# Attention B on features normalized ahead, its projections drained by ScalarE, with new starting ranks for all stages

## Chip, core and metric

The kernel runs on one core of a Trainium2 chip. The metric is the device time of one execution in microseconds (us); the kernel before has a median of 1521.22 us over three runs (1521.19 to 1521.49). The engines are called by the profile's names: PE is TensorE (matmuls, with PEld for its weight loads), DVE is VectorE, ACT is ScalarE, POOL is GpSimd, SP is SyncE, which issues the DMAs.

## The reference

The input x is 4 x 2048 x 256 in float32. Four blocks follow one another, each as x = x + block(layernorm(x)): attention A, the FFN, attention B, and the FFN again. What matters here is attention B, where S (4 here) is its sequence and the 2048 positions are its batch:

```python
k = (src @ Wk_w.T + Wk_b).reshape(S, B, n, -1)
v = (src @ Wv_w.T + Wv_b).reshape(S, B, n, -1)
q = (inp @ Wq_w.T + Wq_b).reshape(S, B, n, -1)
k = unitnorm(k); q = unitnorm(q)
w = sigmoid(src @ Ww_w.T + Ww_b)
A = einsum('sbnq,sbnv->bnvq', k, v * w[:, :, :, None])
r = sigmoid(inp @ Wr_w.T + Wr_b)
out = einsum('sbnq,bnvq->sbnv', q, A) * r[:, :, :, None]
out = out.reshape(S, B, d) @ Wo_w.T + Wo_b
```

with n = 16 heads of 16 numbers. The FFN is 256 to 704 to 256 with silu, and its inputs, weights and hidden values are all rounded blockwise to a 4-bit grid. Attention A divides by norms taken over the whole tensor, so a first pass over all of x has to end before its main pass can begin.

## The kernel before, in words

The 2048 positions are cut into 16 groups of 128 (one position per partition). A group holds its four sequence steps s side by side, `x` [128, 4, 256], and a tile is one (group, s). Each group goes through `attention_a`, `ffn_in` and four `ffn_tile` for the first FFN, `attention_b`, then `ffn_in` and four `ffn_tile` for the second.

Ahead of the groups, `first_pass` loads all x once, takes moments of each tile with `bn_stats` (L653, into a tile `moments` of its own, with sums in `both`), normalizes on ScalarE into four borrowed tiles `XN`, and lets TensorE sum the products of features over all of x (L551). It also loads and prepares the weights: `center` (L903 to L921) subtracts from a weight matrix its mean over the input features. To do so it multiplies the matrix by ones on TensorE (L910), and VectorE subtracts the result divided by 256 from both halves (L916). With centered weights, the mean of x need not be subtracted from x.

Attention B uses this. It takes the sums and variances of x, lets GpSimd work out the reciprocal deviation rstd (`root`, six steps of `take_rstd`; the FFN takes two more for a shift `off`), and transposes the raw x on TensorE (`turn`, L1122, copied out by ScalarE in L1129). For each tile, `project` (L1145) multiplies it by the centered `wqkB` (512 columns) and `wvgB` (288 columns: values and two gates) into two PSUM banks. VectorE drains both in L1528 as bank x rstd + bias, into `qk` and `vg`; the biases lie on all partitions in `bqkB` and `bvgB`, loaded by SP (L484). Then VectorE multiplies all pairs (L1546) and sums over heads (L1553), ScalarE squares (L1577), gates and roots follow, GpSimd weighs the values (L1654), VectorE adds them (L1672, L1675), and the result is turned and projected by `woB`. The bias of the last projection is added to x by GpSimd ahead (L1494), after the transposes have read x.

The FFN tile is TensorE's largest piece: hidden products (L1363), a silu on ScalarE (L1384), the product on VectorE (L1395), the blockwise rounding (`quantize`: VectorE L384, L385, L389, L402, L405, ScalarE L395 and L1192, GpSimd L1220), transposes (L1418, copied by L1430) and the down projection (L1441). `ffn_in` has, for the whole group, `root`, four normalizations on ScalarE (L378) into `xn`, the same rounding, and `turn`. The sums that a next layernorm needs come with the additions to x (L339), and the variances from ScalarE (L345).

The order is written by a planner in the kernel (`Plan`). Each operation is registered with an engine, an estimated duration, a rank, and tokens that it reads and writes. `plan.order(2)` then plays the engines forward in time. Whenever an engine is free, it gets the ready operation of the lowest rank whose buffers are to be had. An operation marked `port=True` is not started while the other of VectorE and GpSimd runs such a one. The result is a fixed instruction order for each engine. `BEGIN` (L1078) gives every group six starting ranks, for attention A, `ffn_in` and tiles of the first FFN, attention B, `ffn_in` and tiles of the second. Buffers come from pools: four banks for hidden products (`mm`), four others (`bank`) for everything else that TensorE writes, eight x, six `turned`, one `qk`, two `vg`. `given` takes a buffer out of a pool for the first pass and returns it after its last user.

Of the kernel before, what the change touches and what calls it, by code (L numbers as in the profile page):

```python
# [18 lines left out]
P = 128  # L19
# [230 lines left out]
def kernel(  # L250
# [56 lines left out]
    def load_x(dst, j):  # L307
# [10 lines left out]
    bqkB = one([P, 2 * D], "bqkB")  # L318
    bvgB = one([P, NV], "bvgB")
# [4 lines left out]
    norm_tiles = {k: one([P, NJ, 6, S], f"norms_{k}") for k in ("a", "f1", "b", "f2")}  # L324


    moments = one([P, NJ, S, 6], "moments")
    both = one([P, NJ, S, 2], "both")
    norms = {
        (k, j): [t[:, j, n, :] for n in range(6)]  # L330
# [26 lines left out]
    def take_rstd(key, step):  # L357
        sums, var, y, off, v, t = norms[key]
        if step == 0:
            nc.gpsimd.tensor_scalar(v, var, 1.0 / D**3, LN_EPS, ALU.mult, ALU.add)  # L360
        elif step == 1:
            power(v, y, nhalf[:, 0, :])
        elif step == 2:
            nc.gpsimd.tensor_mul(t, y, y)
        elif step == 3:
            nc.gpsimd.tensor_mul(t, t, v)
        elif step == 4:
            nc.gpsimd.tensor_scalar(t, t, -0.5, 1.5, ALU.mult, ALU.add)
        elif step == 5:
            nc.gpsimd.tensor_mul(y, y, t)  # L370
        elif step == 6:
            nc.gpsimd.tensor_mul(off, sums, y)
        else:
            nc.gpsimd.tensor_scalar(off, off, -1.0 / D, 0.0, ALU.mult, ALU.add)
# [55 lines left out]
    tiles("tok", 1, [P, S, D], fp)  # L430
    tiles("vz", 2, [P, S, 2 * D], bp)
# [12 lines left out]
    def first_pass():  # L444
# [5 lines left out]
        for b in XN:  # L450
            nc.gpsimd.memset(b.ap[:, :, D : D + 1], 1.0)
        WQK, PROD, WNAT = (plan.given("pp", 0) for _ in range(3))
# [4 lines left out]
        wnat = WNAT.ap.rearrange("p (t c) d -> p t c d", t=2)  # L457
        MK, GROW, MAPT, G = (plan.given(p, 0) for p in ("vz", "tok", "sc", "fac"))
# [32 lines left out]
        for at, token, fn in (  # L491
# [23 lines left out]
            (34.1, ("bB", 0), over_rows(bqkB[:, :D], b_bq)),  # L515
            (34.2, ("bB", 0), over_rows(bqkB[:, D:], b_bk)),
            (34.3, ("bB", 0), over_rows(bvgB[:, :D], b_bv)),
            (34.4, ("bB", 0), over_rows(bvgB[:, D : D + NH], b_br)),
            (34.5, ("bB", 0), over_rows(bvgB[:, D + NH :], b_bw)),
# [54 lines left out]
        def roots(js):  # L574
# [3 lines left out]
            half = [moments[:, js, :, 3 * i + 1 : 3 * i + 3] for i in range(2)]  # L578
            total = both[:, js]
# [45 lines left out]
        for ns in together:  # L625
            for n in ns:
# [21 lines left out]
                for s in range(S):  # L648
# [5 lines left out]
                            moments[:, j, s, :], xj[:, s, :]  # L654
                        ),
                        [(X, s)],
                        [("moments", j, s)],
# [5 lines left out]
            seen = [("moments", i, s) for i in js for s in range(S)]  # L663
# [239 lines left out]
        def center(at, w, n, tokens):  # L903
# [10 lines left out]
            def dve():  # L914
                for c in range(KC):
                    nc.vector.scalar_tensor_tensor(  # L916
                        w[:, c, :], mm.ap[:, :n], -1.0 / D, w[:, c, :], ALU.mult, ALU.add
                    )

            op("PE", 0.2 + n / 290.0, at, pe, tokens, [(mm, 0)])  # L920
            op("DVE", 0.2 + n / 450.0, at + 2, dve, [(mm, 0)], tokens)  # L921
# [16 lines left out]
        center(AHEAD + 50.0, wqkB, 2 * D, [("wqkB", 0)])  # L938
        center(AHEAD + 54.0, wvgB, NV, [("wvgB", 0)])
# [139 lines left out]
        (-91, -18, -64, 57, -73, -13),  # L1079
        (35, 82, 59, 126, 299, 228),  # L1080
        (293, 397, 356, 450, 375, 486),
        (370, 404, 412, 488, 580, 596),
        (433, 471, 475, 573, 630, 638),
        (485, 530, 525, 621, 687, 715),
        (518, 567, 530, 673, 716, 745),
        (588, 644, 630, 743, 560, 676),
        (602, 669, 606, 752, 637, 771),
        (671, 699, 702, 801, 719, 886),
        (714, 797, 826, 891, 958, 1069),
        (788, 865, 877, 996, 972, 1083),  # L1090
        (839, 971, 923, 1030, 822, 1063),
        (879, 1027, 930, 1059, 1017, 1130),
        (910, 1041, 830, 1087, 873, 1230),
        (953, 1023, 1012, 1151, 918, 976),
    ]

    def group(j):
# [7 lines left out]
        def xs(s):  # L1105
            return X.ap[:, s, :]
# [56 lines left out]
        def root(at, key):  # L1163

            n = 6 if key[0] == "b" else 8
# [321 lines left out]
        def attention_b(at):  # L1487
            key = ("b", j)
            root(at, key)
            xT = turn(at, X, range(S), lambda: X.ap)  # L1490

            def bias():
# [8 lines left out]
                at + 3,  # L1501
# [6 lines left out]
            for s in range(S):  # L1508
                a, b = plan.buf("bank"), plan.buf("bank")
                rstd = norms[key][2][:, s : s + 1]  # L1510
                for bank, n, w, bvec, dst, us, ds, name in (
                    (a, 2 * D, wqkB, bqkB, qk, 1.73, 0.7, "wqkB"),
                    (b, NV, wvgB, bvgB, vg, 0.98, 0.46, "wvgB"),
# [10 lines left out]
                        "DVE",  # L1524
                        ds,
                        at + 5 + 3 * s,
                        lambda bank=bank, n=n, bvec=bvec, dst=dst, s=s, rstd=rstd: (
                            nc.vector.scalar_tensor_tensor(  # L1528
                                dst.ap[:, s, :],
                                bank.ap[:, :n],  # L1530
                                rstd,
                                bvec,
                                ALU.mult,
                                ALU.add,
                            )
                        ),
                        [(bank, 0), (key, "rstd"), ("bB", 0)],
# [236 lines left out]
```

## Time and profile before

| | us |
|---|---|
| median of three runs | 1521.22 |
| the profiled execution: its time | 1523.6 |
| the profiled execution: span from the first to the last instruction | 1521.6 |
| granted TensorE clock, mean share | 0.997 |
| POOL busy in the span | 693.2 |
| DMA moved | 27.68 MB, mean 18 GB/s |

The profile is of one execution. Its page lists for each engine the busy time, its share of the span and the count of instructions. The span is also cut into 40 equal slices of 38 us, with the busy share in tenths (9 is 90% or more). In the groups of instructions, L12 is line 12 of the kernel, and `qk<-bank` means that `qk` is written and `bank` read. After the shapes stand the count, the busy time of the group, the mean ns of one, and the idle time of the engine just before these instructions, with what ended it. Matmuls are pipelined and their ends are modelled, so TensorE's busy time is more than its work; the distance between starts tells what one costs. A float32 matmul appears as two instructions.

### The profile page before, as it was taken

To read this page: it belongs to the slowest core of one execution; us is meant where nothing else is said; L and a number is where in the kernel's file an instruction comes from. 1 tells how busy PE (TensorE), PEld (TensorE's weight loads), DVE (VectorE), ACT (ScalarE), POOL (GpSimd) and SP (SyncE) were. 2 spreads that over 40 slices of the span, in tenths; PEclk is the share of its full clock that TensorE was granted. 3 is DMA by queue.
4 is the path that set the end of the run, shared out by engine and by line. 5 is a ranking of instruction groups with operands and counts; after the bars stand their busy time and mean duration, and the time that the engine had idled before them with its cause. 6 is when DMAs were issued, how large, how long until landed. Compare 5 with 4: busy or idle time off the path is not lost.

```text
span 1521.6 us, 18780 instructions
## 1 busy us (share of the span) xinstructions
PE 1499.4 (99%) x6362; PEld 1073.0 (71%) x6362; DVE 1387.3 (91%) x2266; ACT 810.1 (53%) x1745; POOL 693.2 (46%) x750
## 2 busy tenths in 40 slices
PE   7989999999999999999999999999999999999999
PEld 6847676766767666677667676776677677667777
DVE  6899999899899998989999999898989899999985
ACT  6666455555636556455554455465654455445443
POOL 5444454444536254444543543544453644553531
PEclk9999999999999999999999999999999999999999
DMA  8300000000000000000000000100000000000000
GB/s 268 100 1 1 1 1 0 29 0 11 18 4 7 18 4 5 8 4 22 4 18 8 8 21 14 42 5 4 5 7 1 0 1 1 5 11 14 14 22 21
DMA packets 29025, 27.68 MB, mean 18 GB/s; under 512 B 3585, under 2 KB 28673, under 8 KB 28929
## 3 DMA queue, kind: packets, MB, share of 16 engines
q1 hardware_dynamic: 28928, 26.49, 5.6%
q8 instruction: 50, 0.82, 0.2%
q14 instruction: 47, 0.38, 0.1%
HBM read 18.09 MB, written 8.39 MB: 17 GB/s over the span
## 4 chain that ended last, share of the span: by engine, by line
PE 80%; DVE 15%; issue 2%; ACT 1%; DMA 1%; POOL 0%; SPq 0%; DVEq 0%; POOLq 0%; ACTq 0%
PE bank L1363 32%; PE bank L1441 19%; PE bank L1145 18%; PE bank L1418 5%; PE bank L1122 3%; PE bank L551 2%; DVE h L1395 1%; DVE sh L384 1%; DVE pp L1546 1%; DVE qa L402 1%; DVE sc L1553 1%; DVE qa L389 1%; DVE qa L405 1%; DVE fac L1586 1%; DVE qk L1528 1%
## 5 line engine op out<-in xcount | busy, mean ns | idle before, releaser
L1363 PE MATMUL bank<-wguT,turned 128*128 128x352 f32 x2048 | 637.7, 459 | 0.3 <-DVE h L1395 0.3
L1363 PEld LDWEIGHTS bank<-wguT,turned 128*128 128x128 f32 x2048 | 379.7, 190 | 193.8 <-issue 11.7
L1220 POOL TENSOR_TENSOR qa<-qa,sh 128x704 f32<-128x704 f32 x128 | 203.0, 1586 | 407.6 <-DVE qa L405 315.6
L1441 PE MATMUL bank<-wdT,hqT 128*128 128x256 f32 x1536 | 350.6, 380 | 0.4 <-DVE x L1473 0.4
L1441 PEld LDWEIGHTS bank<-wdT,hqT 128*128 128x128 f32 x1536 | 289.5, 190 | 55.6 <-issue 4.5
L1430 ACT COPY hqT<-bank 128x512 f32<-128x512 f32 (+1 forms) x256 | 114.5, 479 | 94.6 <-PE bank L1418 92.4
L1384 ACT ACTIVATE sil<-bank 128x352 f32<-128x352 f32 x256 | 116.1, 458 | 88.9 <-PE bank L1363 83.5
L395 ACT ACTIVATE qm<-qa 128x704 bf16<-128x704 f32 (+1 forms) x136 | 105.9, 781 | 106.4 <-DVE qa L389 103.4
L1395 DVE TENSOR_TENSOR h<-sil,bank 128x352 f32<-128x352 f32 x256 | 128.8, 508 | 19.1 <-PE bank L1363 11.3
L1654 POOL TENSOR_TENSOR pp<-vg,sc 128x1024 f32<-128x1024 f32 x64 | 131.0, 2066 | 31.8 <-DVE tok L1675 27.1
L402 DVE SCALAR_TENSOR_TENSOR qa<-qm,qa 128x704 f32<-128x704 bf16 (+1 forms) x136 | 125.5, 924 | 12.0 <-ACT qm L395 11.9
L389 DVE SCALAR_TENSOR_TENSOR qa<-sh,h 128x704 f32<-128x704 f32 x128 | 126.7, 994 | 2.2
L1145 PE MATMUL bank<-wvz,turned 128*128 128x512 f32 x256 | 119.4, 604 | 5.5 <-ACT turned L1129 4.0
L405 DVE SCALAR_TENSOR_TENSOR qa<-qm,qa 128x704 f32<-128x704 bf16 (+1 forms) x136 | 122.1, 898 | 3.0
L384 DVE TENSOR_REDUCE sh<-h 128x44 f32<-128x748 f32 x128 | 119.1, 931 | 3.7
L1145 PE MATMUL bank<-wqkB,turned 128*128 128x512 f32 x256 | 119.6, 593 | 0.0
L1129 ACT COPY turned<-bank 128x512 f32<-128x512 f32 x160 | 86.8, 588 | 58.3 <-PE bank L1122 58.1
L1418 PEld LDWEIGHTS bank<-ident,qa 128*128 128x128 f32 x768 | 90.7, 141 | 29.0 <-issue 12.0
L1220 POOL TENSOR_TENSOR qax<-qax,sx 128x1024 f32<-128x1024 f32 x32 | 68.3, 2135 | 87.2 <-DVE qax L405 81.8
L1418 PE MATMUL bank<-ident,qa 128*128 128x128 f32 x768 | 105.0, 273 | 1.2 <-POOL qa L1220 1.1
L1192 ACT ACTIVATE sh<-sh 128x44 f32<-128x44 f32 x128 | 30.6, 239 | 119.2 <-DVE sh L384 116.3
L1145 PEld LDWEIGHTS bank<-wvz,turned 128*128 128x128 f32 x256 | 47.2, 193 | 54.3 <-issue 41.5
(180 smaller groups left out, 2150.1 us busy)
## 6 DMA issues: line engine op xcount, KB each, us to landing
x<-in_L_attn_a_x_dram SPq DMA_DIRECT2D x23, 512.0 KB, 5.5
out_dram<-x SPq DMA_DIRECT2D x64, 128.0 KB, 1.7
hqT<-in_L_ffn_w_down_dram SPq DMA_DIRECT2D x2, 352.0 KB, 3.9
hqT<-in_L_ffn_w_gate_dram SPq DMA_DIRECT2D x5, 128.0 KB, 3.9
hqT<-in_L_ffn_w_up_dram SPq DMA_DIRECT2D x5, 128.0 KB, 2.7
x<-in_L_attn_a_x_dram SPq DMA_DIRECT2D x4, 128.0 KB, 2.3
pp<-in_L_attn_a_Wq_dram SPq DMA_DIRECT2D x2, 256.0 KB, 5.6
pp<-in_L_attn_a_Wk_dram SPq DMA_DIRECT2D x2, 256.0 KB, 5.2
```

Of the source, the lines that this page charges most:

```text
L384: nc.vector.tensor_reduce(amax, src, AX.X, ALU.max, apply_absolute_value=True)
L389: nc.vector.scalar_tensor_tensor(blocks(a), over_blocks(rs), -6.0 * BELOW, src, ALU.mult, ALU.mult)
L402: nc.vector.scalar_tensor_tensor(a, m, FLOOR, a, ALU.max, ALU.add)
L405: nc.vector.scalar_tensor_tensor(a, m, FLOOR, a, ALU.max, ALU.subtract)
L1145: nc.tensor.matmul(bank.ap[:, :n], lhs.ap[:, c, s * P : (s + 1) * P], w[:, c, :], start=(c == 0), stop=(c == KC - 1),)
L1220: lambda: nc.gpsimd.tensor_mul(blocks(a.ap), blocks(a.ap), over_blocks(q.ap[:, 1, :])),
L1363: nc.tensor.matmul(bank.ap[:, :HF], xqT.ap[:, c, s * P : (s + 1) * P], w[:, c, cols], start=(c == 0), stop=(c == KC - 1),)
L1384: lambda g=g, sil=sil: nc.scalar.activation(sil.ap, g.ap[:, :HF], AF.Silu),
L1395: lambda u=u, sil=sil, half=half: nc.vector.tensor_mul(h.ap[:, half * FB // 2 : (half + 1) * FB // 2, :BLK], blocks(sil.ap), blocks(u.ap[: ...
L1418: nc.tensor.transpose(bank.ap[:, (i - i0) * P : (i - i0 + 1) * P], qa.ap[:, HC[i] : HC[i] + P], ident,)
L1441: nc.tensor.matmul(o.ap[:, :D], hqT.ap[:, i, :], wdT[:, i, :], start=(i == 0), stop=(i == 5),)
L1654: nc.gpsimd.tensor_mul(pv.ap.rearrange("p t (n e) -> p t n e", e=HD), vg.ap[:, :, :D].rearrange("p t (n e) -> p t n e", e=HD), over_blocks ...
```

## The change

In attention B, ScalarE first normalizes the group's four tiles into a new buffer `xh` (a pool of one). The shift has 1 added to it, so each normalized row has a mean of one. `turn` reads `xh` in place of x. `root` has eight steps here too, as the shift is needed.

`center` now puts the biases into the weights of attention B: the bias, divided by 256 like the mean, is added to every row of the centered matrix. As the features sum to 256, the product contains the bias once. This takes one more VectorE instruction in each of two calls. The bias tiles become buffers lent from the pools `turned` and `fac` for the first pass. The banks of the two projections then need nothing but a copy, and ScalarE makes it in place of VectorE.

To make room in SBUF, the moments of the first pass lie in columns of the fourth borrowed tile, the one of pool `qk`, that its features leave free, and the norm tiles of all layers but the first are shared by groups j and j + 8. The table `BEGIN` has other numbers throughout.

```diff
-    norm_tiles = {k: one([P, NJ, 6, S], f"norms_{k}") for k in ("a", "f1", "b", "f2")}
-    moments = one([P, NJ, S, 6], "moments")
-    both = one([P, NJ, S, 2], "both")
+    norm_tiles = {
+        k: one([P, NJ if k == "a" else NJ // 2, 6, S], f"norms_{k}") for k in ("a", "f1", "b", "f2")
+    }
...
-            nc.gpsimd.tensor_scalar(off, off, -1.0 / D, 0.0, ALU.mult, ALU.add)
+            nc.gpsimd.tensor_scalar(
+                off, off, -1.0 / D, 1.0 if key[0] == "b" else 0.0, ALU.mult, ALU.add
+            )
...
+    tiles("xh", 1, [P, S, D], fp)
...
+        MOMENTS = XN[3]
+        def moments(js):
+            row, first, n = js.start // 4, js.start % 4, js.stop - js.start
+            assert first + n <= 4
+            return [
+                MOMENTS.ap[:, row, at + S * k * first : at + S * k * (first + n)].rearrange(
+                    "p (j s k) -> p j s k", s=S, k=k
+                )
+                for at, k in ((D + 8, 6), (D + 8 + 4 * S * 6, 2))
+            ]
...
+        BIAS, BIAS2 = (plan.given(p, 0) for p in ("turned", "fac"))
+        bqkB = BIAS.ap[:, 0, :]
+        bvgB = BIAS2.ap.rearrange("p i n -> p (i n)")[:, :NV]
...
-        def center(at, w, n, tokens):
+        def center(at, w, n, tokens, bias=None):
...
             def dve():
+                less, part = mm.ap[:, :n], -1.0 / D
+                if bias:
+                    less, part = bias[0], 1.0 / D
+                    nc.vector.scalar_tensor_tensor(
+                        less, mm.ap[:, :n], -1.0, less, ALU.mult, ALU.add
+                    )
                 for c in range(KC):
                     nc.vector.scalar_tensor_tensor(
-                        w[:, c, :], mm.ap[:, :n], -1.0 / D, w[:, c, :], ALU.mult, ALU.add
+                        w[:, c, :], less, part, w[:, c, :], ALU.mult, ALU.add
                     )
...
-        center(AHEAD + 50.0, wqkB, 2 * D, [("wqkB", 0)])
-        center(AHEAD + 54.0, wvgB, NV, [("wvgB", 0)])
+        center(AHEAD + 50.0, wqkB, 2 * D, [("wqkB", 0)], (bqkB, BIAS))
+        center(AHEAD + 54.0, wvgB, NV, [("wvgB", 0)], (bvgB, BIAS2))
...
     BEGIN = [
-        (-91, -18, -64, 57, -73, -13),
-        (35, 82, 59, 126, 299, 228),
-        (293, 397, 356, 450, 375, 486),
...
-        (910, 1041, 830, 1087, 873, 1230),
-        (953, 1023, 1012, 1151, 918, 976),
+        (-180, -233, -93, -411, -178, -161),
+        (30, -17, 75, 47, 270, 251),
+        (165, 222, 216, 279, 209, 381),
...
+        (818, 610, 806, 933, 837, 1624),
+        (833, 730, 831, 1007, 156, 703),
     ]
...
-            n = 6 if key[0] == "b" else 8
+            n = 8
...
         def attention_b(at):
             key = ("b", j)
             root(at, key)
-            xT = turn(at, X, range(S), lambda: X.ap)
+            xh = plan.buf("xh")
+            for s in range(S):
+                op(
+                    "ACT",
+                    0.52,
+                    at + 1.0 + 0.1 * s,
+                    lambda s=s: normalize(xh.ap[:, s, :], xs(s), key, s),
+                    [(X, s), (key, "rstd")],
+                    [(xh, s)],
+                )
+            xT = turn(at + 1.5, xh, range(S), lambda: xh.ap)
...
-                at + 3,
+                at + 6,
                 bias,
...
                     op(
-                        "DVE",
+                        "ACT",
                         ds,
                         at + 5 + 3 * s,
-                        lambda bank=bank, n=n, bvec=bvec, dst=dst, s=s, rstd=rstd: (
-                            nc.vector.scalar_tensor_tensor(
-                                dst.ap[:, s, :],
-                                bank.ap[:, :n],
-                                rstd,
-                                bvec,
-                                ALU.mult,
-                                ALU.add,
-                            )
+                        lambda bank=bank, n=n, dst=dst, s=s: nc.scalar.copy(
+                            dst.ap[:, s, :], bank.ap[:, :n]
                         ),
-                        [(bank, 0), (key, "rstd"), ("bB", 0)],
+                        [(bank, 0)],
                         [(dst, s)],
                     )
```

The planner's durations for the two drains go from 0.7 and 0.46 us to 0.5 and 0.31. The loads of the biases (L484) keep their ranks and their places in the list.

## Prediction

> **What bounds the kernel now.** I read the page's first two parts, then TensorE's own waits, the stages, and the starts of single matmuls.
>
> The page's busy times and its 40 slices:
>
> ```profile
> PE 1499.4 (99%) x6362; PEld 1073.0 (71%) x6362; DVE 1387.3 (91%) x2266; ACT 810.1 (53%) x1745; POOL 693.2 (46%) x750
> ...
> PE   7989999999999999999999999999999999999999
> ```
>
> TensorE is busy in every slice, but ends of matmuls are modelled, so I count its work by the distance from one start to the next. The chain gives 48 matmuls of L1363 in 14.20 us (296 ns each) and 12 of L1441 in 2.59 us (216). In the timeline a 512-wide one starts every 429 ns, a 288-wide one every 243, a 128-wide one every 109, and the first pass's pair (257 and 129 wide) every 329. With the counts of the groups: 2048 x 296 = 606; 1536 x 216 = 332; 526 x 429 = 226; 260 x 243 = 63; 260 x 216 = 56; some 1470 x 109 = 160; 128 x 329 = 42; 1 for the smallest; in all 1486 us. The first matmul starts at 9.96 us, the last ends at 1518.5 of 1521.6, which is 3.1 before the end. So 1521.6 = 10.0 + 1486 + 3.1 + 22.4, and only the 22.4 us lost between matmuls is open to a better order. The same subtraction by stretch puts 4.1 of it in 0 to 40 us, 0.5 in 40 to 80, 8.3 in 80 to 120 and 9.5 in all the rest.
>
> TensorE's waits (total, times, longest) say on whom:
>
> ```profile
> PE bank L551 <- ACT vg L378: 10.0, 1, 10.0
> PE bank L1145 <- ACT turned L1129: 4.0, 1, 4.0
> PE bank L1418 <- POOL qa L1220: 1.1, 2, 0.6
> PE bank L1122 <- DVE x L339: 0.6, 1, 0.6
> PE bank L1145 <- DVE x L339: 0.5, 1, 0.5
> ```
>
> The 10.0 is the start: loads, moments, first normalized tile. The 4.0 is one wait at 108 us, while the first groups fill the machine. The others are short, and stand behind VectorE or behind GpSimd, which stands behind VectorE. The stages (columns: length, then busy time with count of TensorE, its weight loads, VectorE, ScalarE, GpSimd, then the clock) show who was late:
>
> ```profile
> 80.00:120.00 40.00, 35.28 (x108) 17.96 (x107) 37.06 (x68) 26.67 (x56) 21.12 (x27) 0.91 0.00 1
> 120.00:1480.00 1360.00, 1356.58 (x5709) 968.64 (x5708) 1265.07 (x1980) 722.08 (x1557) 629.85 (x613) 1.00 0.03 9
> ```
>
> From 80 to 120 us VectorE is busy 37.1 of 40, and the clock falls to 0.91: after the 4.0 us wait the next 512-wide matmuls start 850 to 1010 ns apart instead of 429, which costs as much again. The first matmuls of all, at 10 to 15 us, are slow in the same way; most of the first 4.1 us is that and stays. The Trainium skill ("TensorE: Matmul & The Clock Gate", section "What's actually happening") says that the array falls to half its clock after an idle window of about 3.4 us and needs a busy one of that length to come back. The rows agree; by that rule a long wait costs double and many short ones only themselves.
>
> So the floor of any reordering is 10.0 + 1486 + 3.1 + about 3.5 = 1502.6 us of span, 19 below now.
>
> **The change, part by part.**
>
> *VectorE loses two drains per tile.* The two forms of L1528:
>
> ```profile
> L1528 DVE SCALAR_TENSOR_TENSOR qk<-bank,norms_b,bqkB 128x512 f32<-128x512 f32 x64 | 46.8, 737 | 13.9 <-PE bank L1145 13.6
> L1528 DVE SCALAR_TENSOR_TENSOR vg<-bank,norms_b,bvgB 128x288 f32<-128x288 f32 x64 | 32.1, 503 | 3.6 <-PE bank L1145 1.8 <-POOL norms_f L372 1.0 <-POOL norms_b L370 0.2
> ```
>
> 46.8 + 32.1 = 78.9 us go, less 1.1 for one extra instruction in each of two `center` calls (681 and 446 ns, the rows of L916). Busy falls from 1387 to 1310, 91% to 86%. From 120 to 1480 us VectorE's idle time rises from 95 to about 174 us. None of it is on the path by itself: the matmuls cover it.
>
> *ScalarE takes them, and four normalizations per group.*
>
> ```profile
> L1129 ACT COPY turned<-bank 128x512 f32<-128x512 f32 x160 | 86.8, 588 | 58.3 <-PE bank L1122 58.1
> L378 ACT ACTIVATE xn<-x,norms_f 128x256 f32<-128x256 f32 x128 | 68.6, 593 | 31.3 <-POOL norms_f L374 25.8 <-DVE qax L389 5.6
> ```
>
> 64 x 588 = 37.6; the 288-wide copy lies between L1430's 373 ns (256 wide) and L822's 474 (384), about 398, so 64 x 398 = 25.5; 64 x 593 = 38.0. That is 101 us by duration. In sequence they start closer (four normalizations take 2.07 us), so about 85 us more busy: 895 us, 59%. Cost on the path: nothing, while ScalarE has 638 us idle between 120 and 1480.
>
> *GpSimd takes two more steps per group's root*, 16 x 2 x about 0.32 = 10 us (mean of L372 and L374), 46% still. Hidden. TensorE's matmuls keep count and shape. The bias loads keep size and number; but the last one, issued at 53.4 us and landing 2.6 later, is now needed by the last `center`, whose matmuls start at 63.3 us: 7 us in hand, so 0, and at worst the same 7 us if SP's queue slips. Moments in another tile: same instructions, 0 (up to 0.4 us each if a load arrives behind it).
>
> *A wait is added.* Attention B's transposes read raw x now, behind VectorE's last sum. After the change they wait for variance (0.5 + 0.2 us), eight root steps (2.95 us from first to last at 100.6) and four normalizations (2.07), some 5.7 us. Behind a late transpose TensorE's whole queue stands. Ends: 0, and 16 x 5.7 = 91 us with no cover; there is no end below 0, since this wait relieves nobody. I take 0. The nearest row is the FFN input, which has this very chain and quantization after it 32 times, and all idle time before its transposes is:
>
> ```profile
> L1122 PE MATMUL bank<-ident,qax 128*128 128x128 f32 x256 | 34.8, 278 | 0.6 <-DVE x L339 0.6
> ```
>
> The cover is other groups' FFN tiles: eight x buffers, each group's FFN tiles some 32 us of matmuls per layer.
>
> *The order is remade.* BEGIN has new numbers everywhere, so every engine's order changes, and no row prices that. Bounds: 19 us better (the floor) and, the other way, the 91 above.
>
> What I take: the 9.5 us lost after 120 us falls by two thirds, 6 us, since nearly all of it stands behind VectorE, whose slack there nearly doubles; the 8.3 of the fill is VectorE-bound too, but no attention B runs there, so I credit 1 us. 1521.6 - 7 = 1514.6 of span. The profiled execution took 1523.6 us outside a span of 1521.6; the median of the runs is 1521.2, 0.4 under that span. So 1514.2, **1514 us**.
>
> **A rule that speaks against it.** Laying the two engines' records side by side, 45 of 64 `vg` drains and 44 of 64 `qk` drains had GpSimd at work for over half their time, and took the same (501 against 509, 736 against 737 ns). L389, with both inputs in SBUF, took 1190 ns there against 892 without. So the drains that go are work that lost nothing to GpSimd, and what stays, does. The Trainium skill ("SBUF — State Buffer", section "SBUF: two separate sides") gives the reason: a VectorE instruction with two SBUF inputs and a GpSimd instruction lock each other out of a shared port pair. By that rule the 79 us freed can only partly be used, the late stalls stay, and the sum would be 1521.
>
> **Rivals.**
> 1. *The fill goes too.* If the new order leaves no wait over 1 us between 80 and 120 us, the clock stays up, and about 8 us more go: 1514 - 8 = 1506. For it: one wait makes it all. Against: VectorE has 2.9 us idle in those 40.
> 2. *The change buys nothing that TensorE can use.* VectorE's and GpSimd's shared instructions bind as before, the waits move but keep their sum: 1521. For it: the long SBUF instructions and GpSimd's 693 us are untouched. Against: non-contending work (L384, L1395) is plentiful and can fill in.
> 3. *Slower: the transposes of attention B come late.* The normalizations queue in ScalarE behind a table load (1283 ns), a square (1056) and copies, and TensorE stands. One such delay is about 1 us per group; 16 groups, 16 us; less the 6 gained, 1531. It decides from 7/16 = 0.44 us per group. One wait of 4 us, with the slow clock behind it, counts 8. For it: ScalarE's 85 us more, in strict order with 58 table loads. Against: the 0.6 us above.
>
> **How the numbers follow.** Forecast (1510 to 1518) 0.41; rival 1 (1503 to 1510) 0.16; rival 2 (1518 to 1525) 0.15; rival 3 (1525 to 1545) 0.28. The last is taken to 1531, its price; together with the bottom left out below 1504 that leaves under 2 in 10. Range 1504 to 1531. This kernel's measurement can tell 0.2%, 3 us, from no change. Faster by more: rival 1 and all of the forecast, 0.57; within: 0.14; slower: 0.29.
>
> **What would show it.** Right: VectorE at 1310, ScalarE at 895, TensorE's waits after 120 us under 4 us in total, the sum of starts still 1486. Step by step: no idle time before `bank<-ident,xh` over 1 us in all; ScalarE's copies of `qk` and `vg` at 588 and 398 ns. Wrong: a TensorE wait on the normalizations or on `turned` of 2 us or more, a clock under 0.97 in a slice after 120 us, or more table loads than 58. What would break the forecast above all is the fill: its wait can double or go, 8 us either way, and nothing in this profile fixes it.

## The result, and the profile after

The kernel after takes 1524.02 us (median of 22 runs, 1522.12 to 1526.70), the kernel before 1521.57 us beside it (22 runs). The ratio is 1.0016 with an interval of 1.0009 to 1.0022: a faster kernel is excluded, and the loss of 2.5 us is smaller than the 0.2% that the prediction took as its measure. One of the 22 runs of before lay far off, at 2266.8 us, and is not in the ratio.

The profiled execution took 1523.4 us, its span is 1521.3. The first two parts of the page after, to be held against the same lines of before:

```profile
PE 1499.4 (99%) x6362; PEld 1072.7 (71%) x6362; DVE 1345.6 (88%) x2140; ACT 894.8 (59%) x1937; POOL 709.1 (47%) x782
...
PE   7999999999999999999999999999999999999999
```

The work has moved as the diff says: 126 instructions fewer on VectorE, 192 more on ScalarE. TensorE's waits after (total, times, longest) have a new list:

```profile
PE bank L570 <- ACT vg L378: 8.3, 2, 8.0
PE bank L1173 <- DVE wvz L1076: 2.4, 1, 2.4
PE bank L1173 <- ACT turned L1157: 2.1, 2, 1.9
PE bank L1446 <- POOL qa L1248: 1.5, 3, 1.1
PE bank L1446 <- ACT vg L1564: 0.9, 2, 0.7
...
PE bank L1446 <- ACT hqT L1458: 0.5, 1, 0.5
PE bank L1446 <- ACT qk L1564: 0.4, 1, 0.4
```

In place of one wait of 4.0 us in the fill stand two, of 2.4 (at 72 us) and 1.9 (at 113 us). The short waits on VectorE's additions to x are gone, and the FFN's transposes (L1446, L1418 before) wait for ScalarE's copies instead. The stages after (columns as in the prediction):

```profile
80.00:120.00 40.00, 37.69 (x117) 18.19 (x116) 37.83 (x73) 25.29 (x56) 21.58 (x33) 1.00 0.02 8
120.00:1480.00 1360.00, 1355.29 (x5711) 969.05 (x5710) 1222.99 (x1853) 808.74 (x1750) 645.35 (x639) 1.00 0.03 9
```

From 80 to 120 us TensorE is better off, but after 120 us it has 1.3 us less busy time, although VectorE has 42 us more idle time there.

The prediction's ledger can be drawn up for every run: for each matmul the distance to the next start, less the usual distance of its shape (the one that it has when nothing delays it, 296 ns for 352 columns). The sum of these usual distances is about 1485.5 us in every kernel here, the tail 3.2. What differs (us):

| run | first matmul | lost 0-40 | 40-120 | after 120 | VectorE busy | span | time, median | ratio to before, interval |
|---|---|---|---|---|---|---|---|---|
| before | 10.0 | 4.2 | 8.9 | 9.6 | 1387 | 1521.6 | 1521.57 | |
| b_again | 8.3 | 4.7 | 8.1 | 9.7 | 1388 | 1519.8 | 1521.8 | |
| after | 8.0 | 5.1 | 8.1 | 11.1 | 1346 | 1521.3 | 1524.02 | 1.0016, 1.0009-1.0022 |
| a_again | 8.5 | 4.8 | 9.9 | 11.9 | 1346 | 1524.1 | 1526.2 | |
| b_act_drain | 7.9 | 5.0 | 7.9 | 8.5 | 1339 | 1518.3 | 1520.50 | 0.9993, 0.9984-1.0002 |
| a_dve_drain | 8.4 | 4.4 | 7.7 | 51.4 | 1409 | 1560.8 | 1562.78 | 1.0273, 1.0259-1.0287 |
| b_seed0 | 8.1 | 4.7 | 5.8 | 39.5 | 1402 | 1547.1 | 1548.53 | 1.0179, 1.0149-1.0209 |
| a_old_seed0 | 7.4 | 4.9 | 10.1 | 33.9 | 1352 | 1545.3 | 1547.55 | 1.0172, 1.0143-1.0202 |
| b_seed1 | 8.7 | 5.2 | 8.4 | 46.1 | 1402 | 1557.3 | 1558.02 | 1.0241, 1.0212-1.0271 |
| a_old_seed1 | 8.5 | 5.5 | 8.0 | 40.0 | 1352 | 1551.0 | 1552.08 | 1.0202, 1.0173-1.0232 |
| a_join_first | 8.1 | 4.9 | 7.9 | 11.3 | 1346 | 1521.2 | 1523.36 | 1.0013, 1.0004-1.0022 |
| a_fit | 9.3 | 3.6 | 6.0 | 16.5 | 1349 | 1524.4 | 1526.01 | 1.0031, 1.0019-1.0043 |
| b_fit | 8.0 | 3.8 | 5.4 | 17.1 | 1397 | 1523.3 | 1524.74 | 1.0020, 1.0011-1.0029 |
| a_cal | 8.6 | 7.0 | 7.1 | 15.6 | 1342 | 1527.2 | 1529.34 | 1.0049, 1.0036-1.0062 |
| b_cal | 8.4 | 8.9 | 8.7 | 16.6 | 1384 | 1531.6 | 1533.43 | 1.0075, 1.0061-1.0090 |
| a_half_pool | 8.2 | 4.4 | 8.2 | 9.6 | 1325 | 1519.4 | 1521.94 | 1.0002, 0.9994-1.0011 |
| a_split | 8.1 | 4.1 | 10.5 | 16.2 | 1337 | 1527.8 | 1527.51 | 1.0038, 1.0024-1.0052 |
| a_copies_first | 8.3 | 4.0 | 9.3 | 9.8 | 1341 | 1520.6 | 1521.84 | 1.0001, 0.9992-1.0010 |
| a_both | 7.9 | 4.6 | 7.9 | 9.7 | 1341 | 1519.1 | 1521.46 | 1.0000, 0.9991-1.0009 |
| a_all | 10.2 | 3.7 | 9.0 | 12.7 | 1345 | 1524.6 | 1523.92 | 1.0015, 1.0006-1.0024 |

Names with b_ are made from before, with a_ from after. The ledger is of one execution, the median of several; in every execution the time is some 2 us above the span. The first profile of before flattered the comparison of spans: its first matmul came 1.7 us later than in the second.

### The profile page after: what moved, and what is told of

It reads as the page before. It is cut to its first block, busy times and chain, and to the rows that moved or that the text cites. A ratio compares the mean times of both kernels' runs of the same rounds, so it can differ in the third digit from the quotient of the medians.

```text
span 1521.3 us, 18876 instructions
## 1 busy us (share of the span) xinstructions
PE 1499.4 (99%) x6362; PEld 1072.7 (71%) x6362; DVE 1345.6 (88%) x2140; ACT 894.8 (59%) x1937; POOL 709.1 (47%) x782
## 4 chain that ended last, share of the span: by engine, by line
PE 85%; DVE 9%; ACT 2%; issue 2%; POOL 1%; DMA 1%; SPq 0%; POOLq 0%; DVEq 0%; ACTq 0%
PE bank L1391 34%; PE bank L1173 20%; PE bank L1469 19%; PE bank L1446 5%; PE bank L1150 4%; PE bank L570 2%; DVE qa L402 1%; DVE h L1423 1%; DVE sh L384 1%; DVE qa L405 1%; DVE qa L389 1%; POOL qa L1248 1%; DVE sh L385 0%; DMA x<-in_L_attn_a_x_dram 0%; PE bank L930 0%
## 5 line engine op out<-in xcount | busy, mean ns | idle before, releaser
L1248 POOL TENSOR_TENSOR qa<-qa,sh 128x704 f32<-128x704 f32 x128 | 206.0, 1610 | 393.4 <-DVE qa L405 295.1
L395 ACT ACTIVATE qm<-qa 128x704 bf16<-128x704 f32 (+2 forms) x136 | 105.8, 783 | 94.2 <-DVE qa L389 91.4
L402 DVE SCALAR_TENSOR_TENSOR qa<-qm,qa 128x704 f32<-128x704 bf16 (+2 forms) x136 | 135.1, 994 | 16.6 <-ACT qm L395 16.6
L389 DVE SCALAR_TENSOR_TENSOR qa<-sh,h 128x704 f32<-128x704 f32 x128 | 129.9, 1020 | 2.9
L405 DVE SCALAR_TENSOR_TENSOR qa<-qm,qa 128x704 f32<-128x704 bf16 (+2 forms) x136 | 126.4, 930 | 2.8
L1248 POOL TENSOR_TENSOR qax<-qax,sx 128x1024 f32<-128x1024 f32 x32 | 66.7, 2084 | 120.7 <-DVE qax L405 97.2
L1446 PEld LDWEIGHTS bank<-ident,qa 128*128 128x128 f32 x768 | 90.6, 141 | 33.6 <-issue 13.5
L1446 PE MATMUL bank<-ident,qa 128*128 128x128 f32 x768 | 106.8, 274 | 3.5 <-POOL qa L1248 1.5
L1576 DVE TENSOR_TENSOR pp<-qk 128x1024 f32<-128x1024 f32 x64 | 80.0, 1252 | 9.4 <-ACT qk L1564 9.3
```

Of the source, the lines that this page charges most:

```text
L389: nc.vector.scalar_tensor_tensor(blocks(a), over_blocks(rs), -6.0 * BELOW, src, ALU.mult, ALU.mult)
L402: nc.vector.scalar_tensor_tensor(a, m, FLOOR, a, ALU.max, ALU.add)
L405: nc.vector.scalar_tensor_tensor(a, m, FLOOR, a, ALU.max, ALU.subtract)
L1248: lambda: nc.gpsimd.tensor_mul(blocks(a.ap), blocks(a.ap), over_blocks(q.ap[:, 1, :])),
L1446: nc.tensor.transpose(bank.ap[:, (i - i0) * P : (i - i0 + 1) * P], qa.ap[:, HC[i] : HC[i] + P], ident,)
```

## The experiments

### The two kernels again

Neither is edited; each is run once more for a second profile.

> The kernel before, unedited, for a second profile. If the first profile, whose execution took 2 us over the median, was typical, the first matmul starts near 10 us again. If its start was late by chance, the first matmul starts near 8 us, the span is near 1519.5 us, and TensorE waits longer than 0.3 us for wvz near 72 us.

> The changed kernel, unedited, for a second profile. Theory 1 (two waits during the fill, near 72 and 113 us, let the clock fall for a varying time) expects these two waits again within 0.5 us of 2.4 and 1.9 us, and any difference in time from the first profile to lie in the slow matmuls behind them and in the start of the first matmul.

The late loss repeats: 9.6 and 9.7 us before, 11.1 and 11.9 after, in the same places. The fill of after does not: it is 8.1 and 9.9.

### Drains alone, and drains undone

The theory in the prediction is that VectorE's load causes the late loss. The rival is that the loss belongs to the order. The change has two parts that can be tried apart: the relief without the new ranks, and the new ranks without the relief. In b_act_drain, ScalarE does the drains in the order of before, without the biases:

```diff
-    nc.vector.scalar_tensor_tensor(dst.ap[:, s, :], bank.ap[:, :n], rstd, bvec, ALU.mult, ALU.add)
+    nc.scalar.activation(dst.ap[:, s, :], bank.ap[:, :n], AF.Identity, scale=rstd)
```

> The kernel before in its own order, with one edit: ScalarE drains the two projections of attention B (bank times rstd), VectorE no longer does; the biases are left out, the weights stay as they are. VectorE's busy time must fall by about 79 us as in the change. Theory 1 (the short TensorE stalls come from the fixed order and from GpSimd, not from VectorE's load): within 0.2% of before, 1518.5 to 1524.6 us, losses between matmuls after 120 us still 8 to 11 us. Theory 2 (the relief is worth 6 us and the new order gives it back): 1514 to 1517 us, losses after 120 us under 5 us.

In a_dve_drain, VectorE does the copies in the order of after:

```diff
-                        lambda bank=bank, n=n, dst=dst, s=s: nc.scalar.copy(
+                        lambda bank=bank, n=n, dst=dst, s=s: nc.vector.tensor_copy(
```

> The changed kernel in its own order, with one edit: VectorE instead of ScalarE copies the two projections out of their banks. VectorE's busy time must rise by about 60 us. Theory 1 (order, not load): within 0.3% of the changed kernel, 1520 to 1528 us. Theory 2 (the relief is worth time): 6 us or more over the changed kernel, 1530 us and up, with new TensorE waits behind VectorE.

The relief alone brought 1.1 us after 120 us (9.6 to 8.5), and a time that cannot be told from before: the old order had next to nothing to gain from it. Taking the relief back from the new order cost 40 us there. One reading is that the new ranks had already spent it. Another is that an order planned for copies on ScalarE suits no other placement, since another draw of the ranks alone costs 30 to 37 us (below). These runs do not part the two.

Place by place: before has 57 gaps of over 0.05 us after 120 us, and its repeat has the same 57. In b_act_drain 18 of them (3.2 us) are gone, 39 stay (6.3 us, now 6.5), and 1.8 us are new. Twelve of the 57 are over 0.2 us (5.3 us together), with the same lengths within 15 ns in the repeat. VectorE ended seven of these (3.3 us), GpSimd five. With the relief five of the twelve are gone or shorter (2.4 us less), six are unchanged, three of them behind VectorE, one grew by 0.5, and three are new (1.9 us). The largest new one, in its timeline (start, length, engine, and in brackets the wait and who ended it):

```profile
409.91 1.05 ACT L1572 ACTIVATE pp<-qk 128x1024 f32<-128x1024 f32 x1
410.85 1.58 ACT L378 ACTIVATE xn<-x,norms_f 128x256 f32<-128x256 f32 x3
...
412.33 0.68 ACT L1528 ACTIVATE qk<-bank,norms_b 128x512 f32<-128x512 f32 x1
...
413.06 0.66 PE L1418 MATMUL bank<-ident,qa 128*128 128x128 f32 x4 [0.77 <-ACT qk L1528]
```

The drain of `qk` stands in ScalarE's queue behind a square and three normalizations, its bank comes back late, and the next user of that bank is a transpose of the FFN.

### Orders that nobody chose

`plan.order(n)` adds a small random number (spread 0.7) to every rank, drawn from seed n; 0 adds none, and both kernels use 2. The kernels with seeds 0 and 1 have orders near those on record but not picked. The a_old ones have the work of after with the `BEGIN` of before.

```diff
-    order = plan.order(2)
+    order = plan.order(0)
```

> The kernel before with another small noise on its ranks (seed 0 in place of 2), so its table BEGIN no longer fits and the order is an ordinary one. Theory 1 (both orders were fitted to their durations until TensorE was covered, so the relief has nothing left to buy; it would buy time in an order that is not fitted): 1535 to 1560 us, TensorE losing 25 us or more after 120 us, behind VectorE and GpSimd. Theory 2 (VectorE's load is not what makes TensorE wait in any order): the loss is no larger than the fitted order's 10 us by more than 5.

> The changed kernel's work with the old table and seed 0, an order fitted to neither. Theory 1: faster than the old work with seed 0 by 3 to 12 us, by smaller losses after 120 us. Theory 2: the same within 2 us, or slower.

> As with seed 0, with seed 1: a second ordinary order of the old work. Theory 1: 1535 to 1565 us.

> The changed kernel's work with the old table and seed 1. Theory 1: faster than the old work with seed 1 by 3 to 12 us. Theory 2: the same within 2 us, or slower.

Another draw costs 30 to 37 us after 120 us, three to four times the whole late loss of before. The late loss is smaller with the work of after in both pairs, 33.9 against 39.5 and 40.0 against 46.1. These 5.6 and 6.1 us are near what the prediction credited, as if the relief paid in an order where VectorE is often late. That is a hint and not shown: there are two pairs with two executions of each kernel, the orders of a pair are not the same, and one kernel's two draws lie 6.6 and 6.1 us apart. In time the first pair differs by only 1.0 us, as its fill took back 4.3 of the 5.6, the second by 5.9.

### The wait at 72 us

The plan of after puts the first joined weights (L1075, L1076) behind a block maximum of `w_down` (L704) that waits for its load. a_join_first moves this maximum behind the joins:

```diff
     order = plan.order(2)
+    order.remove(312)
+    order.insert(order.index(370) + 1, 312)
```

> The changed kernel with one VectorE operation moved: the joining of attention A's weights (L1075, L1076) goes ahead of a block maximum of w_down (L704) that stands before it in VectorE's queue and waits for a DMA; the order of all else is kept. Theory 1 (what is lost between matmuls is lost by the order, and 1.4 us of the 2.4 us wait near 72 us by this one place): the wait falls to about 1.0 us, the clock falls less behind it, and the time goes down by 1.4 to 3.5 us, to 1520.5 to 1522.7 us. Theory 3 (the fill as a whole is bound by VectorE, so a wait that goes here comes back near 113 us): no change over 0.5 us.

The wait fell from 2.4 to 1.0 us, the loss from 40 to 120 us by 0.2, and the time by 0.7, which these intervals cannot tell from nothing. So this wait is not shown to make after slower, but it goes with the scatter of its times. Of the 22 runs of after, the ten with a mean clock of 0.999 or more took 1522.1 to 1523.5 us, the twelve below that 1523.95 to 1526.70. a_join_first has no run below 0.999, and its range is 2.7 us in place of 4.6. The same instructions, the windows from 76 to 80 us (columns as in the stages; the first number after POOL is the clock), in the profile of after:

```profile
76.00:80.00 4.00, 4.00 (x9) 1.73 (x8) 3.90 (x9) 0.94 (x2) 1.55 (x1) 0.80 0.11 20
```

and in its repeat a_again:

```profile
76.00:80.00 4.00, 4.00 (x6) 1.51 (x5) 3.86 (x11) 0.79 (x1) 1.55 (x1) 0.50 0.08 13
```

After one and the same wait of 2.4 us the clock is 0.80 once and 0.50 once. The 0.80 is a mean: in finer windows the clock is 0.50 from 74.2 to 77.5 us and 1.00 behind it, and in the repeat 0.50 from 73.4 to 80.2. So the slow spell lasted some 3.4 us once and 6.8 us once. In the repeat the clock also falls behind the second wait (0.50 from 117.8 to 121.1), in the first profile it does not. The Trainium skill ("TensorE: Matmul & The Clock Gate", section "What's actually happening") has windows of 3.4 us that run freely, not set off by the kernel. The two lengths agree with such windows. The page also has the clock fall after an idle window of that length; here waits of 2.4 and 1.9 us were enough, and the measurement decides.

### Plans fitted harder

If the order decides, a better fit should win. a_fit and b_fit have new numbers in `BEGIN` and a correction to the rank of each of 571 and 587 operations, searched with the planner alone; its own end, no measurement, fell by 7.8 us for the work of after and by 4.5 for that of before. In a_cal and b_cal the search was made anew after setting the planner's durations nearer to the trace:

```diff
-    SYNC = 0.08
+    SYNC = 0.15
+    LONGER = {"PE": 0.994, "DVE": 1.02, "ACT": 1.02, "POOL": 1.06, "SP": 1.0}
...
-            dict(engine=engine, us=us, rank=rank, fn=fn, bufs=bufs, port=port, table=table,
+            dict(engine=engine, us=us * self.LONGER[engine], rank=rank, fn=fn, bufs=bufs, port=port, table=table,
...
+    for i, more in MORE.items():
+        plan.ops[i]["rank"] += more
     order = plan.order(2)
```

The last three lines are those of a_fit and b_fit too.

> The changed kernel's work with another order: BEGIN has new numbers and 571 operations, nearly all of the first 140 us, get a rank of their own. The planner's own end falls by 7.8 us against its order for the changed kernel. Theory 1: the loss from 40 to 120 us falls from 8 to 10 us to 3 us or less, the loss after 120 us stays at 9 to 12, and the time is 1514 to 1518 us. Theory 3 (VectorE-bound fill): the loss from 40 to 120 us stays at 7 us or more and the time over 1520 us.

> The old work with another order, found in the same way with the same effort: 587 operations with ranks of their own. The planner's own end falls by 4.5 us against its order for the kernel before. Theory 1: 1516 to 1519 us, the loss from 40 to 120 us at 4 us or less, 1 to 4 us slower than the changed kernel's work fitted alike. Theory 2 (relief of VectorE has no worth in any fitted order): no difference over 1 us between the two.

> The changed kernel's work in an order made with durations nearer the chip's: in the planner VectorE and ScalarE 2% longer, GpSimd 6% longer, matmuls 0.6% shorter, 0.15 us in place of 0.08 from one engine to another; BEGIN and 556 ranks found anew. Theory 4 (the loss after 120 us is what a fixed order pays where the chip differs from the durations it was made with): that loss falls below 7 us, from 11.5 in the changed kernel and 16.5 in the order fitted to the old durations, and the time is 1513 to 1519 us. If it stays at 10 us or more, the loss has another cause.

> The old work, made in the same way with the same longer durations and the same effort; the planner's own end is 12.8 us later than for the changed work, as VectorE, with 79 us more, no longer keeps up in the plan itself. Theory 4 expects 1522 to 1536 us, the loss after 120 us at 10 to 18 us, now behind VectorE as planned. If it comes within 3 us of the changed work's order, the relief of VectorE is worth nothing in an order made for the chip's durations.

All four are slower. With a_fit and b_fit the fill improved as planned (6.0 and 5.4 us lost between 40 and 120), but the loss after 120 us rose to about 17, with the relief as without it. Better mean durations did not help either (15.6 and 16.6), so the theory that the planner's mean durations are to blame fell. Within each pair the relief takes 0.6 and 1.0 us off the late loss; in time the first pair goes the other way (1526.0 and 1524.7), the second parts by 4.1 us. One place in a_cal shows what no mean can hold:

```profile
603.36 6.54 POOL L1685 TENSOR_TENSOR pp<-vg,sc 128x1024 f32<-128x1024 f32 x3
...
605.49 2.62 DVE L390 SCALAR_TENSOR_TENSOR qa<-sh,h 128x704 f32<-128x704 f32 x1
```

Three of GpSimd's value products stand in a row, and beside them an instruction of VectorE that takes 0.89 us elsewhere takes 2.62. The next of its kind takes 2.18, and behind them in VectorE's queue stands the addition to x that ends a TensorE wait of 4.4 us.

### GpSimd beside VectorE

a_half_pool computes only the first half of each of those products; their count stays:

```diff
-                        pv.ap.rearrange("p t (n e) -> p t n e", e=HD),
+                        pv.ap[:, :2].rearrange("p t (n e) -> p t n e", e=HD),
```

a_split does all of them, and the scaling in `quantize`, as two instructions of half the size:

```diff
+                    for t in (0, 2):
+                        nc.gpsimd.tensor_mul(
+                            pv.ap[:, t : t + 2].rearrange("p t (n e) -> p t n e", e=HD),
...
```

> The changed kernel in its own order; GpSimd's weighing of the values (64 instructions of 1024 columns) does only the first half of its columns, so half of the values are left out. VectorE's and TensorE's work is unchanged. Theory 5 (what TensorE loses late comes from GpSimd and VectorE holding each other up, an order that the plan has otherwise): GpSimd's busy time falls by about 65 us, VectorE's by 5 us or more without an instruction less, the loss after 120 us from 11.5 to 8 us or less, the time by 2 to 5 us. If the loss stays at 10 us or more, GpSimd's hold is not what costs.

> The changed kernel in its own order; each of GpSimd's weighings of values (1024 columns) and of its scalings in the rounding (704 and 1024 columns) is made as two instructions of half the columns. Same work. Theory 5: VectorE is held for at most one half, so its busy time falls by 10 us or more; the loss after 120 us falls by 1 to 4 us if the 224 extra instructions of GpSimd (some 0.1 us each by the distance of its small ones) do not take it back. A rise of the time by 5 us or more would say that GpSimd's own length is what TensorE waits for.

With GpSimd at 644 us in place of 709, VectorE's busy time falls by 20 us without one instruction less, the late loss from 11.1 to 9.6, not to the 8 that was expected, and the time by about 2 us. A new wait of 1.3 us, at 396 us behind VectorE, takes part of the gain back. One of the late waits of after can be followed. The timeline of after:

```profile
1430.97 6.37 POOL L1684 TENSOR_TENSOR pp<-vg,sc 128x1024 f32<-128x1024 f32 x3
...
1435.61 2.47 DVE L389 SCALAR_TENSOR_TENSOR qa<-sh,h 128x704 f32<-128x704 f32 x1
...
1442.00 1.39 POOL L1248 TENSOR_TENSOR qa<-qa,sh 128x704 f32<-128x704 f32 x1 [4.66 <-ACT sil L1412]
...
1443.44 0.88 PE L1446 MATMUL bank<-ident,qa 128*128 128x128 f32 x6 [1.05 <-POOL qa L1248]
```

and that of a_half_pool, the same three products and the same L389:

```profile
1430.94 3.74 POOL L1684 TENSOR_TENSOR pp<-vg,sc 128x512 f32<-128x512 f32 x3
...
1434.71 0.89 DVE L389 SCALAR_TENSOR_TENSOR qa<-sh,h 128x704 f32<-128x704 f32 x1
```

There L389 takes 0.89 us, and the gap of 1.2 us at L1446 is gone. In after the three products end at 1437.3 and L389 0.7 us later, as if it had begun only then. GpSimd itself stood idle for 4.7 us before the scaling L1248 that TensorE waits for, so here its own length is not the cause, but what it did to VectorE. Splitting is no way out: VectorE's busy time fell by 8 us, but GpSimd's total rose to 760 us, TensorE's waits on the scaling of `qa` from 1.5 to 5.4 us, and the late loss to 16.2.

### The copies in ScalarE's queue

The other new late waits are those of L1446 on ScalarE, 1.8 us. The timeline of after shows their kind:

```profile
191.33 0.56 ACT L1564 COPY qk<-bank 128x512 f32<-128x512 f32 x1
...
191.92 1.06 ACT L1607 ACTIVATE pp<-qk 128x1024 f32<-128x1024 f32 x1
...
192.89 0.38 ACT L1564 COPY vg<-bank 128x288 f32<-128x288 f32 x1
...
193.32 0.44 PE L1446 MATMUL bank<-ident,qa 128*128 128x128 f32 x2 [0.66 <-ACT vg L1564]
```

The product for `vg` is done, but its copy stands behind a square of 1.06 us, and TensorE wants the bank. a_copies_first changes the finished order: a drain directly behind a square or a variance goes ahead of it. a_both adds the edit of a_join_first (the block maximum goes behind the joins; the expectation words it the other way round). a_all also moves the copies of `hqT` ahead of squares and gates.

```diff
+    acts = [i for i in order if plan.ops[i]["engine"] == "ACT"]
+    for i in list(acts):
+        if not {"bank", "dst", "n"} <= set(line(i).co_varnames):
+            continue
+        n = acts.index(i)
+        late = acts[n - 1]
+        calls = line(late).co_name == "square" or "take_var" in line(late).co_freevars
+        if calls and min(map(order.index, plan.ops[late]["then"])) > order.index(i):
+            order.remove(late)
+            order.insert(order.index(i) + 1, late)
+            acts[n - 1], acts[n] = i, late
```

> The kernel after, with one rule applied to ScalarE's finished order: where a drain copy of the projections (L1564) stands directly behind a square (L1607) or a variance (L342), the two change places; 45 positions move, nothing else. Theory that the new late waits are drains queued behind such work: TensorE's waits on vg, qk and hqT after 120 us (1.8 us in the kernel after) fall below 0.6, the loss after 120 us from 11.1 to about 9.5, the time by 1.5 to 2 us, to about 1522. Rival, that these waits are only where VectorE's lateness shows: the squares and variances that now come later make VectorE or GpSimd wait, the loss after 120 us stays at 11 or rises, 1524 or more.

> The kernel after with both local edits of its order: the block maxima of w_down before the weights for the joined values are prepared (as in the run a_join_first), and the drain copies ahead of squares and variances. If the two losses are separate, their gains add: about 1 us of the fill and 1.5 of the late loss, so 1521.5 to 1522, equal to the kernel before. If only the late one counts, 1522 to 1522.5; if neither, 1523.5 to 1524.5. In no case faster than before by 0.2%.

> As a_both, and in ScalarE's order the copies of hqT (L1458) too go ahead of a square (L1607) or gate (L1626) directly in front of them, and the drains past more than one such step; TensorE's, VectorE's and GpSimd's orders are those of a_both. Theory that the late loss which the change added is bank copies queued in ScalarE behind work that no matmul needs soon: the 1.2 us wait of L1446 on hqT near 191 us goes, the loss after 120 us falls from 9.7 to about 8.5, the span from 1519.1 to about 1518, the time to about 1520.5, 1 us under the kernel before. Rival, that VectorE then lacks the squares: L1616 late, the loss stays at 9.7 or rises, 1521.5 to 1522.5.

a_copies_first did as its theory said: no wait on `vg` or `qk` is left after 120 us, the late loss is 9.8, and the ratio to before falls from 1.0016 to 1.0001. One thing was missed: the waits on `hqT` grew from 0.5 to 1.2 us, as the squares went where the drains had stood. With a_both the fill loses 1.4 us less than in a_copies_first, but its median differs from it by only 0.4 us, less than can be told. a_all took that one wait on `hqT` at 191 us from 1.2 to 0.2 us, and lost: the late loss rose to 12.7, with TensorE waiting elsewhere.

```profile
PE bank L1150 <- POOL qax L1248: 1.9, 2, 1.6
...
PE bank L1469 <- ACT hqT L1458: 0.9, 2, 0.7
```

The 1.6 us, at 257 us, are the input of an FFN whose quantization comes late. So the rival on record for a_all, that the loss does not fall, was right in its sign and too low in its number. Its reason, that VectorE then lacks the squares, holds at this place. VectorE's sum over the squares (L1616) in a_both:

```profile
235.20 1.22 DVE L1616 TENSOR_REDUCE fac<-pp 128x64 f32<-128x1024 f32 x1 [0.34 <-ACT pp L1607]
```

and the same instruction in a_all:

```profile
240.17 1.22 DVE L1616 TENSOR_REDUCE fac<-pp 128x64 f32<-128x1024 f32 x1 [2.23 <-ACT pp L1607]
```

VectorE does the same instructions in the same order in both, and stays late from there to the FFN input at 257 us. The best of the versions with the change, a_both, equals before; none is shown to beat it.

## Why the prediction was wrong

**Right.** ScalarE's sum: 894.8 us for 895. GpSimd's: 709 for 693 + 10, hidden as costed. TensorE's work: the same 1485.5. The copies and the added wait before the transposes, in the groups after:

```profile
L1564 ACT COPY qk<-bank 128x512 f32<-128x512 f32 x64 | 37.0, 584 | 37.7 <-PE bank L1173 37.1 <-DVE pp L1576 0.6
...
L1564 ACT COPY vg<-bank 128x288 f32<-128x288 f32 x64 | 25.3, 396 | 27.9 <-PE bank L1173 27.8
```

```profile
L1150 PE MATMUL bank<-ident,xh 128*128 128x128 f32 x128 | 17.3, 273 | 0.0
```

584 and 396 ns for 588 and 398, and no idle time before the transposes of `xh`. Rival 3's place was therefore wrong: the normalizations are in time. Its cause, ScalarE's strict order, was real, but at the other end of attention B, where the copies give the banks back. The prediction had put the copies' cost on the path at nothing because ScalarE has 638 us idle; idle time in sum says nothing of a bank that waits 1 us behind a square.

**The step that failed** is "the 9.5 us lost after 120 us falls by two thirds, 6 us, since nearly all of it stands behind VectorE, whose slack there nearly doubles". In its place the loss rose from 9.6 to 11.1. What the runs show is, first, that the loss of before stood in some sixty fixed places of its order, and VectorE's relief removed few of them: 1.1 us net in b_act_drain. The profile of before would have told as much. Its waits after 120 us hold 2.1 us behind VectorE and 1.1 behind GpSimd, and the first are, beside the two rows on L339 in the prediction:

```profile
PE bank L1441 <- DVE x L1473: 0.4, 2, 0.2
PE bank L1145 <- DVE x L1473: 0.3, 1, 0.3
PE bank L1363 <- DVE h L1395: 0.3, 1, 0.3
```

So 6 us were more than what stood behind VectorE, and its share of busy time, 91%, said nothing of that. Second, the moved drains queue behind squares and variances: undoing that gives 1.3 us of the late loss back, and the time of before (a_copies_first). What the new ranks did with VectorE's slack stays open: the loss of 51.4 us in a_dve_drain says that the new order needs it, or that it suits no other placement. That the relief would be worth 6 us in an order not fitted to the load is a hint from two pairs of orders.

**VectorE's size.** It fell by 41.7 us, not 77. Summed by duration, its records fell from 1508.9 to 1456.3 us, 52.6; 78.9 went and 1.1 came, so the rest grew by 25. The remaining 11 us are that the records of one engine overlap (by 121.6 us before, 110.6 after): the prediction allowed for that on ScalarE and forgot it on VectorE. In b_act_drain, where the order is that of before, the rest grew by 20, so most of it comes with the relief and not with the new ranks. The largest growth is in groups with two inputs in SBUF. Before:

```profile
L402 DVE SCALAR_TENSOR_TENSOR qa<-qm,qa 128x704 f32<-128x704 bf16 x130 | 121.7, 937 | 12.0 <-ACT qm L395 11.9
L405 DVE SCALAR_TENSOR_TENSOR qa<-qm,qa 128x704 f32<-128x704 bf16 x130 | 118.4, 911 | 2.9
...
L1675 DVE TENSOR_TENSOR tok<-pp 128x256 f32<-128x256 f32 x64 | 29.5, 461 | 1.1
```

and after:

```profile
L402 DVE SCALAR_TENSOR_TENSOR qa<-qm,qa 128x704 f32<-128x704 bf16 x130 | 131.2, 1011 | 16.6 <-ACT qm L395 16.6
...
L405 DVE SCALAR_TENSOR_TENSOR qa<-qm,qa 128x704 f32<-128x704 bf16 x130 | 122.6, 944 | 2.7
...
L1705 DVE TENSOR_TENSOR tok<-pp 128x256 f32<-128x256 f32 x64 | 35.9, 560 | 1.2
```

In after, L402 takes 1239 ns where GpSimd works over half its time (43 of 130) and 898 elsewhere; before it was 1054 (40 of 130) and 885. The drains that went had lost nothing to GpSimd, as the prediction itself had noted. The Trainium skill ("SBUF — State Buffer", section "SBUF: two separate sides") describes an exclusive lock, held for a whole instruction; L389's 2.47 us beside three products in a row agrees. The sum that the prediction drew from that rule, 1521, was nearer to the measured 1524.0 than its own 1514.

**The fill.** The 1 us credited there did not come: 8.9 and 8.1 us were lost from 40 to 120 us before, 8.1 and 9.9 after. One wait of 4 us became two of about 2, and each was followed by the slow clock in at least one of two profiles.

**The rivals.** Rival 2, waits that keep their sum with the shared instructions unchanged, is nearest in time (1518 to 1525 holds 1524.0) and in kind. What it lacked is the new waits on the copies. The range, 1504 to 1531, holds the result, but only through the rivals: by the forecast's own steps the kernel had to be faster.

**Open.** Not every late gap was followed to its cause; the largest left in a_both are 1.4 us at 191 us and the 1.2 us behind the locked L389. The planner already keeps GpSimd's products and VectorE's instructions of this kind apart (`port=True`), so the collisions shown are places where the chip has left the plan. Whether an order that holds them apart on the chip too would let the relief pay was not tried.

## What to carry over

In an order picked for its load, the lost time stands in a few fixed places: list these gaps one by one, and credit a relief at most with those that the relieved engine ends; here three of seven stayed even so. When a drain moves to another engine, price it by what stands directly ahead of it in that engine's queue at the moment the bank is wanted, and move the copy ahead of work that no matmul needs soon, but look who needs that work (a_all). Removing an engine's uncontended instructions can free less than their sum of durations: here what stayed became longer by 25 us beside the other engine's long ones.

## What the runs showed of the hardware

In the places followed, VectorE's instructions with two SBUF inputs did not lengthen by a share: 0.89 us became 2.47 and 2.62 beside three GpSimd products in a row, the 2.47 until 0.7 us after the last product had ended. Halving these products took 20 us off VectorE's busy time (1345.6 to 1325.3) at an unchanged count of 2140.

A TensorE wait of 2.4 us, at the same place of the same program, was followed by a clock of 0.50 for some 3.4 us in one execution and for some 6.8 us in another.
